# Spreading softmax weights three neighbours at a time in row groups of TensorE, with products and sums on tiles of three

## The chip, the cores and the metric

The kernel runs on one core of a Trainium2 chip. The metric is the device time of one execution in microseconds (us); the runs of the kernel before took 6155.91, 6143.2 and 6156.27, median 6155.91.

## What is computed

The input is x of 16 images, 56 x 56 pixels, 384 channels, all float32. Two layers follow each other; each adds its result to its input. Before each, a group norm over 32 groups of 12 channels is taken for the whole image. The first layer is a dilated neighbourhood attention: 384 channels are three sets of 128 (dilation 1, 2 and 3), each of four heads of 32 channels, and every pixel attends to nine neighbours.

```python
xn = gn(x);  qkv = einsum('bchw,oc->bohw', xn, w_qkv)      # q, k, v for three dilations d = 1, 2, 3
for each dilation d, head h, pixel n:
    attn[n, k] = sum_c q[c, n] * k[c, n + d*(ky-1, kx-1)] * 32**-0.5     # k = 3*ky + kx, nine neighbours
    attn = softmax over k
    out[c, n]  = sum_k attn[n, k] * v[c, n + d*(ky-1, kx-1)]
x = x + einsum(out, w_proj) + b_proj
x = x + depthwise_3x3(gn(x), sign(clip(w_conv)))           # second layer
```

## The kernel before

**Tiles and stages.** An image is seven chunks of eight rows (448 pixels); there are 112 chunks. Channels lie on the 128 partitions, pixels on the free axis. Three plans work on a chunk at different times. Stage A (`plan_a`) loads x, transposes it (L304), takes statistics and stores the transposed copy in DRAM. Stage B (`plan_b`) is the attention with its output projection. Stage C (`plan_c`) is the convolution and the transposition back.

**Order.** Time is divided into steps, nine to a chunk (`STEP`, L579). `at(when, order, piece)` files each piece of work under a step and a kind (L578: SOFTMAX, SCORE, CONVOLVE, WEIGH, QUERY, QKV, PROJECT, ...), and the pieces are issued in that order. Stage A runs nine chunks ahead of B, C ten behind. Each engine has one queue, in order; the framework fixes the order of the instructions of each engine when the kernel is built, and it may let a later piece pass one that isn't ready: in the trace, the third spread matmul of a step often stands among the projection matmuls that follow it. `in_one_go` (L225) keeps the matmuls of a burst together.

**Stage B of a chunk**, with t0 as its first score step:

- `k_or_v` (L341) projects k and v (L337) and copies them from PSUM with ScalarE into `kv` tiles with a border (L346). K and V share a tile, of which there are three per dilation (`KV_SLOTS`). The rows of the border come from the neighbouring chunk by DMA on the SP queue (L350, L351).
- `score` (L378), steps t0 to t0+8: one VectorE product q x k for three neighbours at once (tile t, 128 x 1344, L387). The products of four neighbours are summed over channels by matmuls of 128 rows and 32 columns (L371), which run in four column groups of the array at once, as do the convolution's (L553).
- `softmax_1`, `softmax_2`, `softmax_3` at t0+9 to t0+11: the scores are transposed by a permutation matrix (L400) to 112 pixels by 108 weights, four times; maximum, difference, exponential, sum, reciprocal and product run on VectorE and ScalarE (L405 to L415) with the nine neighbours innermost. `softmax_3` splits each weight into three bf16 terms, alternating between ScalarE and GpSimd (L422 to L425).
- `turn_weights` (L427), t0+12 to t0+14: for each dilation, four transposes (L430) give a tile of 108 rows (three terms x four heads x nine neighbours) and ScalarE copies it (L436).
- `weigh` (L438), t0+13 to t0+21, three neighbours per step: one bf16 matmul with the matrix `spread` (108 rows, 128 columns, L443) sums the terms of a neighbour's weights and copies each to its head's 32 partitions; VectorE multiplies the result, in PSUM, by the shifted v (L446); GpSimd adds the product to y (L453), eight adds per dilation.
- `out_project` (L459), t0+23 to t0+25: projection of the three y (L467), bias and residual on VectorE (L470), statistics (L473), store.

**Norms.** Once per image and layer, `group_stats` and `spread_stats` (L232 to L273) pass small tiles between TensorE, VectorE and ScalarE in a chain.

**PSUM** has eight banks: four for the shared tag "mt" (projections, transposes, convolution, norms), one for the query, one for the scores, and two for the spread weights ("bc").

```python
pb = ps_bc.tile([P, 512], F32, tag="bc", name="pb_a")
nc.tensor.matmul(pb[:, :PX], spread[:, o, :], had[f"a{g}"], start=True, stop=True)
w = w_p.tile([P, PX], F32, tag="w", name="w")
vw = kv[g][slot][:, 1, ky * d : ky * d + ROWS, kx * d : kx * d + W]
nc.vector.tensor_tensor(rows(w), rows(pb[:, :PX]), vw, ALU.mult)
```

Of the kernel before, what the change touches and what calls it, by code (L numbers as in the profile page):

```python
# [8 lines left out]
F32 = mybir.dt.float32  # L9
BF16 = mybir.dt.bfloat16  # L10
AF = mybir.ActivationFunctionType
# [13 lines left out]
GN_CH = 12  # L25
GN_G = 32
NR = NG * HEADS * NTAP
KV_SLOTS = 3
TERMS = 3


# [1 line left out]
def dilated_attention_then_binary_conv(  # L33
# [34 lines left out]
    DIL = (1, 2, 3)  # L68
    K3 = 3 * HD

    xf = x.rearrange("b h w c -> b (h w) c")
    of = out.rearrange("b h w c -> b (h w) c")

    const = ctx.enter_context(tc.tile_pool(name="const", bufs=1))
    ps_mt = ctx.enter_context(tc.tile_pool(name="ps_mt", bufs=4, space=PSUM))
    ps_q = ctx.enter_context(tc.tile_pool(name="ps_q", bufs=1, space=PSUM))
    ps_s = ctx.enter_context(tc.tile_pool(name="ps_s", bufs=1, space=PSUM))
    ps_bc = ctx.enter_context(tc.tile_pool(name="ps_bc", bufs=2, space=PSUM))


    ident = const.tile([P, P], F32, name="ident")
# [9 lines left out]
    for h in range(HEADS):  # L91
        nc.gpsimd.memset(sel[h * HD : (h + 1) * HD, SEL0 + h : SEL0 + h + 1], 1.0)

    perm = const.tile([P, NG, HEADS, NTAP], F32, name="perm")
    nc.gpsimd.memset(perm, 0.0)
    for p in range(NG * NTAP):
        g, o = divmod(p, NTAP)
        nc.gpsimd.affine_select(
            out=perm[:, g, :, o], in_=perm[:, g, :, o], compare_op=ALU.not_equal, fill=1.0,
            base=-(32 * (p % 4) + 4 * (p // 4)), pattern=[[-1, HEADS]], channel_multiplier=1,  # L100
        )
    permf = perm.rearrange("p g h o -> p (g h o)")


    gsel = const.tile([P, NG, GN_G], F32, name="gsel")
# [16 lines left out]
    wprojT = const.tile([P, NG, C], F32, name="wprojT")  # L122
    bias = const.tile([P, NG], F32, name="bias")

    spread = const.tile([NR, NTAP, P], BF16, name="spread")

    kdiag = const.tile([K3, 3, NG * NQ, HD], F32, name="kdiag")
    with tc.tile_pool(name="setup", bufs=1) as setup:
# [28 lines left out]
        nc.tensor.transpose(pt[:, :NG], b_in, ident[:NG, :NG])  # L157
        nc.vector.tensor_copy(bias, pt[:, :NG])

        spread_f = setup.tile([NR, NTAP, P], F32, name="spread_f")  # L160
        nc.gpsimd.memset(spread_f, 0.0)
        for t in range(TERMS):
            nc.gpsimd.affine_select(
                out=spread_f.rearrange("r o (h d) -> r o h d", h=HEADS),
                in_=spread_f.rearrange("r o (h d) -> r o h d", h=HEADS),
                compare_op=ALU.not_equal, fill=1.0, base=-t * HEADS * NTAP,
                pattern=[[-1, NTAP], [-NTAP, HEADS], [0, HD]], channel_multiplier=1,
            )
        nc.vector.tensor_copy(spread, spread_f)


# [28 lines left out]
    xn_p = ctx.enter_context(tc.tile_pool(name="xn_p", bufs=3))  # L200
    xr_p = ctx.enter_context(tc.tile_pool(name="xr_p", bufs=2))
    t_p = ctx.enter_context(tc.tile_pool(name="t_p", bufs=3))
    w_p = ctx.enter_context(tc.tile_pool(name="w_p", bufs=5))
    y_p = ctx.enter_context(tc.tile_pool(name="y_p", bufs=5))
    s_p = ctx.enter_context(tc.tile_pool(name="s_p", bufs=1))
    a_p = ctx.enter_context(tc.tile_pool(name="a_p", bufs=4))
    z_p = ctx.enter_context(tc.tile_pool(name="z_p", bufs=3))
    x1_p = ctx.enter_context(tc.tile_pool(name="x1_p", bufs=2))
    o_p = ctx.enter_context(tc.tile_pool(name="o_p", bufs=2))
# [1 line left out]


    kv = []
    for g, d in enumerate(DIL):
        kv.append([])
        for s in range(KV_SLOTS):
            t = const.tile([P, 2, ROWS + 2 * d, W + 2 * d], F32, name=f"kv_{g}_{s}")
            nc.gpsimd.memset(t[:, :, :, 0:d], 0.0)
            nc.gpsimd.memset(t[:, :, :, W + d : W + 2 * d], 0.0)
            kv[g].append(t)  # L220

    def rows(ap):
        return ap.rearrange("p (r w) -> p r w", w=W)

    def in_one_go(matmuls):  # L225

# [54 lines left out]
    def at(when, order, piece):  # L281

        pieces.setdefault((when, order), []).append(piece)
# [37 lines left out]
    def plan_b(m, t0):  # L321

        b, c = divmod(m, NCH)
        slot, prev = m % KV_SLOTS, (m - 1) % KV_SLOTS
        had = {}

        def load_x():
# [12 lines left out]

        def k_or_v(g, which):  # L341

            d, cur, bef = DIL[g], kv[g][slot][:, which], kv[g][prev][:, which]
            pk = ps_mt.tile([P, 512], F32, tag="mt", name="pkv")
            project(pk, (1 + which) * C + g * P)
            nc.scalar.copy(cur[:, d : d + ROWS, d : d + W], rows(pk[:, :PX]))  # L346
            if c == 0:
                nc.gpsimd.memset(cur[:, 0:d, :], 0.0)
            else:
                nc.sync.dma_start(cur[:, 0:d, :], bef[:, ROWS : ROWS + d, :])  # L350
                nc.sync.dma_start(bef[:, ROWS + d : ROWS + 2 * d, :], cur[:, d : 2 * d, :])  # L351
            if c == NCH - 1:
                nc.gpsimd.memset(cur[:, ROWS + d : ROWS + 2 * d, :], 0.0)
# [24 lines left out]
        def score(i):  # L378

            g, ky = divmod(i, 3)  # L380
            d = DIL[g]
            qg = rows(had["q"][:, :PX])
            q3 = bass.AP(qg.tensor, qg.offset, [qg.ap[0], (0, 3), *qg.ap[1:]])
            kw = kv[g][slot][:, 0, ky * d : ky * d + ROWS, 0:W]
            k3 = bass.AP(kw.tensor, kw.offset, [kw.ap[0], (d, 3), *kw.ap[1:]])
            t = t_p.tile([P, 3, PX], F32, tag="t", name="t")
            nc.vector.tensor_tensor(t.rearrange("p k (r w) -> p k r w", w=W), q3, k3, ALU.mult)  # L387
            ready.extend((i * 3 + kx, t[:, kx, :]) for kx in range(3))
            if len(ready) >= NQ or i == 8:
                score_round()  # L390

        NH = NSUB * NG * HEADS

        def softmax_1():

# [2 lines left out]
            pt = ps_mt.tile([P, 512], F32, tag="mt", name="pt_s")  # L398
            for s in range(NSUB):
                nc.tensor.matmul(  # L400
                    pt[:SUB, s * NR : (s + 1) * NR], sT[:, s * SUB : (s + 1) * SUB], permf, start=True, stop=True
                )
            pt3 = pt[:SUB, : NSUB * NR].rearrange("p (h o) -> p h o", o=NTAP)
            mx = s_p.tile([SUB, NH], F32, tag="mx", name="mx")
            nc.vector.reduce_max(mx, pt3, axis=AX.X)  # L405
            had["e"] = e = s_p.tile([SUB, NH, NTAP], F32, tag="e", name="e")
            nc.vector.tensor_tensor(e, pt3, mx.unsqueeze(2).to_broadcast([SUB, NH, NTAP]), ALU.subtract)
            nc.scalar.activation(e, e, AF.Exp, scale=SCALE)

        def softmax_2():  # L410
            e = had["e"]
            sm = s_p.tile([SUB, NH], F32, tag="sm", name="sm")
            nc.vector.reduce_sum(sm, e, axis=AX.X)
            nc.vector.reciprocal(sm, sm)
            nc.vector.tensor_tensor(e, e, sm.unsqueeze(2).to_broadcast([SUB, NH, NTAP]), ALU.mult)  # L415

        def softmax_3():

            ef = had.pop("e").rearrange("p (s h) o -> p s (h o)", s=NSUB * NG)
            had["e3"] = e3 = s_p.tile([SUB, NSUB * NG, TERMS, HEADS * NTAP], BF16, tag="e3", name="e3")  # L420
            rest = s_p.tile([SUB, NSUB * NG, HEADS * NTAP], F32, tag="rest", name="rest")
            nc.scalar.copy(e3[:, :, 0], ef)  # L422
            nc.gpsimd.tensor_tensor(rest, ef, e3[:, :, 0], ALU.subtract)  # L423
            nc.scalar.copy(e3[:, :, 1], rest)
            nc.gpsimd.tensor_tensor(e3[:, :, 2], rest, e3[:, :, 1], ALU.subtract)  # L425

        def turn_weights(g):  # L427
            pa = ps_mt.tile([P, 1024], BF16, tag="mt", name="pa")
            for s in range(NSUB):
                nc.tensor.transpose(  # L430
                    pa[:NR, s * SUB : (s + 1) * SUB],
                    had["e3"][:, s * NG + g].rearrange("p t m -> p (t m)"),
                    ident_h[:SUB, :SUB],
                )
            had[f"a{g}"] = aT = a_p.tile([NR, PX], BF16, tag="aT", name="aT")
            nc.scalar.copy(aT, pa[:NR, :PX])  # L436

        def weigh(p):  # L438

            g, o = divmod(p, NTAP)  # L440
            d, (ky, kx) = DIL[g], divmod(o, 3)
            pb = ps_bc.tile([P, 512], F32, tag="bc", name="pb_a")
            nc.tensor.matmul(pb[:, :PX], spread[:, o, :], had[f"a{g}"], start=True, stop=True)  # L443
            w = w_p.tile([P, PX], F32, tag="w", name="w")
            vw = kv[g][slot][:, 1, ky * d : ky * d + ROWS, kx * d : kx * d + W]
            nc.vector.tensor_tensor(rows(w), rows(pb[:, :PX]), vw, ALU.mult)  # L446
            if o == 0:
                had["w0"] = w
                return
            if o == 1:  # L450
                had[f"y{g}"] = y_p.tile([P, PX], F32, tag="y", name="y")
            y = had[f"y{g}"]
            nc.gpsimd.tensor_tensor(y, had["w0"] if o == 1 else y, w, ALU.add)  # L453

        def load_residual():
            had["xr"] = xr = xr_p.tile([P, NG, PX], F32, tag="xr", name="xr")
# [37 lines left out]
        at(t0 + 9, SOFTMAX, softmax_1)  # L494
        at(t0 + 10, SOFTMAX, softmax_2)
        at(t0 + 11, SOFTMAX, softmax_3)
        for g in range(NG):
            at(t0 + 12 + g, SOFTMAX, lambda g=g: turn_weights(g))
        for p in range(NG * NTAP):
            at(t0 + 13 + p // 3, WEIGH, lambda p=p: weigh(p))  # L500
        at(t0 + 19, LOADS, load_residual)
        for j in range(NG):
            at(t0 + 23 + j, PROJECT, lambda j=j: out_project(j))
# [111 lines left out]
```

## Time and profile before

| what | value |
|---|---|
| median of the three runs | 6155.91 us |
| profiled execution's own time | 6148.66 us |
| its span, first to last instruction | 6146.7 us |
| mean granted TensorE clock | 0.961 |
| busy: TensorE matmul | 5892.8 us (96%) |
| busy: VectorE | 4420.6 us (72%) |
| busy: GpSimd | 3364.3 us (55%) |
| busy: ScalarE | 2270.5 us (37%) |
| DMA queue q1, share of 16 engines | 48.8% |
| spread matmuls L443 | 3024, 929.5 us busy, 360 ns each |
| products with v, L446 | 3024, 1797.4 us busy, 616 ns each |
| adds to y, L453 | 2688, 3057.9 us busy, 1137 and 1139 ns each |
| transposes of weights, L430 | 1344, 139.9 us busy |

The busy time of an engine counts each moment once, so overlapping matmuls add up to less than count times duration. Matmuls are pipelined: the duration of a row contains the way through the array, and the distance from one start to the next is what a matmul keeps the engine. PEld is the loading of weights, which overlaps with matmuls. The first spread matmul starts 157 us after the span's beginning and the last ends at 5948 us; before and after that only stages A and C and the setup have work.

### The profile page before, as it was taken

What the parts mean: (1) busy time and instruction counts of PE and PEld (TensorE: products, weight loads), DVE (VectorE), ACT (ScalarE), POOL (GpSimd) and SP (SyncE); (2) the same over time, 40 slices, a digit from 0 to 9 for tenths busy, and PEclk for the clock granted to TensorE, in tenths of its full rate; (3) what the DMA queues carried; (4) which work ended last, traced back from release to release, by engine and by line L of the source; (5) the groups of instructions that cost most, each with busy time, mean ns of one, the idle gap of its engine ahead of it and who ended that gap; (6) DMA issues with size and microseconds to landing.
All of it is one profiled execution on the core that took longest, in us unless ns stands there. A gap on an engine that the chain in (4) does not pass through costs nothing. (4 is left out here: it accounts for less than half of the span.)

```text
span 6146.7 us, 90026 instructions
## 1 busy us (share of the span) xinstructions
PE 5892.8 (96%) x30933; PEld 2720.9 (44%) x30933; DVE 4420.6 (72%) x6431; ACT 2270.5 (37%) x4025; POOL 3364.3 (55%) x3375
## 2 busy tenths in 40 slices
PE   6989999999999999999999999999999999999986
PEld 3434444444444444444444444444444444444432
DVE  3767777777777777777777777777777777777760
ACT  2222333333333333334333333333334333333334
POOL 1656555555555555555555556555555555555650
PEclk7999999999999999999999999999999999999985
DMA  4323445554555455545554555555455554444445
GB/s 149 105 69 102 138 132 150 147 148 141 140 149 146 136 152 141 146 136 147 152 143 137 142 148 142 143 146 148 140 140 149 150 149 139 133 131 115 125 131 143
DMA packets 675072, 848.03 MB, mean 138 GB/s; under 512 B 179507, under 2 KB 674614, under 8 KB 674614
## 3 DMA queue, kind: packets, MB, share of 16 engines
q1 hardware_dynamic: 670608, 841.67, 48.8%
q8 instruction: 244, 4.00, 0.3%
q14 instruction: 214, 1.75, 0.1%
q10 hardware_dynamic: 4006, 0.61, 0.1%
HBM read 539.11 MB, written 231.21 MB: 125 GB/s over the span
## 5 line engine op out<-in xcount | busy, mean ns | idle before, releaser
L453 POOL TENSOR_TENSOR y<-y,w 128x448 f32<-128x448 f32 x2352 | 2675.0, 1137 | 1227.8 <-DVE w L446 1085.8
L446 DVE TENSOR_TENSOR w<-pb_a,kv 128x448 f32<-128x448 f32 x3024 | 1797.4, 616 | 479.0 <-PE pb_a L443 468.4
L337 PE MATMUL pkv<-xn,wqkvT 128*128 128x448 f32 x4032 | 1641.9, 542 | 0.0
L387 DVE TENSOR_TENSOR t<-pq,kv 128x1344 f32<-128x1344 f32 x1008 | 1545.9, 1547 | 86.6 <-PE pq L337 70.2
L337 PEld LDWEIGHTS pkv<-xn,wqkvT 128*128 128x128 f32 x4032 | 762.2, 190 | 622.7 <-issue 592.7
L536 ACT ACTIVATE z<-z,mrz 96x448 f32<-96x448 f32 x1344 | 939.2, 757 | 124.7 <-DMA z<-x1d 99.2
L553 PE MATMUL pc<-z,kdiag 96*32 96x440 f32 (+1 forms) x8064 | 924.3, 561 | 54.2 <-ACT z L536 32.0
L443 PE MATMUL pb_a<-aT,spread 108*128 108x448 bf16 x3024 | 929.5, 360 | 47.9 <-DVE w L446 38.5
L346 ACT COPY kv<-pkv 128x448 f32<-128x448 f32 x672 | 358.6, 534 | 1607.8 <-PE pkv L337 1607.4
L337 PE MATMUL pq<-xn,wqkvT 128*128 128x448 f32 x2016 | 904.5, 560 | 0.0
L467 PE MATMUL po<-y,wprojT 128*128 128x448 f32 x2016 | 828.6, 539 | 1.7 <-POOL y L453 1.7
L371 PE MATMUL ps<-t,sel 128*32 128x448 f32 x6048 | 781.1, 570 | 31.7 <-DVE var L255 15.9
L453 POOL TENSOR_TENSOR y<-w 128x448 f32<-128x448 f32 x336 | 382.9, 1139 | 724.6 <-DVE w L446 685.7
L560 DVE TENSOR_TENSOR x<-pc,x 128x448 f32<-128x448 f32 x336 | 209.8, 624 | 582.6 <-PE pc L553 581.9
L443 PEld LDWEIGHTS <-spread 108*128 108x128 bf16 x3024 | 238.0, 98 | 786.7 <-issue 730.1
L467 PEld LDWEIGHTS po<-y,wprojT 128*128 128x128 f32 x2016 | 382.1, 190 | 337.3 <-issue 305.8
L470 DVE SCALAR_TENSOR_TENSOR xr<-po,bias,xr 128x448 f32<-128x448 f32 x336 | 228.7, 681 | 407.5 <-PE po L467 401.8
L337 PEld LDWEIGHTS pq<-xn,wqkvT 128*128 128x128 f32 x2016 | 400.1, 200 | 260.8 <-issue 230.2
L553 PEld LDWEIGHTS pc<-z,kdiag 96*32 96x32 f32 x8064 | 265.7, 113 | 554.3 <-issue 463.3
L423 POOL TENSOR_TENSOR rest<-e,e 112x432 f32<-112x432 f32 x112 | 114.2, 1019 | 391.4 <-ACT e L422 375.1
L308 ACT COPY xa<-pt_x 128x448 f32<-128x448 f32 x336 | 179.0, 534 | 362.5 <-PE pt_x L304 355.0
L333 ACT ACTIVATE xn<-xn,mr 128x448 f32<-128x448 f32 x336 | 231.4, 751 | 202.8 <-DMA xn<-xd 145.9
(90 smaller groups left out, 3363.0 us busy)
## 6 DMA issues: line engine op xcount, KB each, us to landing
z<-x1d SPq DMA_DIRECT2D x912, 224.0 KB, 4.0
xin<-in_x_dram SPq DMA_DIRECT2D x112, 672.0 KB, 6.5
xd<-xa SPq DMA_DIRECT2D x336, 224.0 KB, 2.3
xn<-xd SPq DMA_DIRECT2D x112, 672.0 KB, 4.5
xr<-xd SPq DMA_DIRECT2D x112, 672.0 KB, 4.3
x1d<-xr SPq DMA_DIRECT2D x112, 672.0 KB, 3.1
x<-x1d SPq DMA_DIRECT2D x112, 672.0 KB, 5.0
out_dram<-osb SPq DMA_DIRECT2D x448, 168.0 KB, 2.3
```

Of the source, the lines that this page charges most:

```text
L333: nc.scalar.activation(xj, xj, AF.Identity, bias=mr0[b][:, j, 0:1], scale=mr0[b][:, j, 1:2])
L337: nc.tensor.matmul(dst[:, :PX], wqkvT[:, cc, o0 : o0 + P], had["xn"][:, cc, :], start=(cc == 0), stop=(cc == NG - 1))
L346: nc.scalar.copy(cur[:, d : d + ROWS, d : d + W], rows(pk[:, :PX]))
L371: return nc.tensor.matmul(had["ps"][32 * j : 32 * j + 32, :PX], sel[:, s0 : s0 + 32], tk, start=(i == 0), stop=(p + NQ >= NG * NTAP),)
L387: nc.vector.tensor_tensor(t.rearrange("p k (r w) -> p k r w", w=W), q3, k3, ALU.mult)
L443: nc.tensor.matmul(pb[:, :PX], spread[:, o, :], had[f"a{g}"], start=True, stop=True)
L446: nc.vector.tensor_tensor(rows(w), rows(pb[:, :PX]), vw, ALU.mult)
L453: nc.gpsimd.tensor_tensor(y, had["w0"] if o == 1 else y, w, ALU.add)
L467: nc.tensor.matmul(po[:, :PX], wprojT[:, g, j * P : (j + 1) * P], had[f"y{g}"], start=(g == 0), stop=(g == NG - 1))
L470: nc.vector.scalar_tensor_tensor(xr[:, j, :], po[:, :PX], bias[:, j : j + 1], xr[:, j, :], op0=ALU.add, op1=ALU.add)
L536: nc.scalar.activation(z[:, q], z[:, q], AF.Identity, bias=mr1[b][:, j, q, 0:1], scale=mr1[b][:, j, q, 1:2])
L553: return nc.tensor.matmul(pcr[q * HD : (q + 1) * HD, :, lo:hi], kdiag[:, kx, j * NQ + q, :], rows(z[:, q])[:, :, lo + kx - 1 : hi + kx - 1 ...
```

## The change

For each dilation and each of its three rows of neighbours (ky), the three neighbours kx are now handled together:

- The weights of a chunk are laid out by neighbour, then dilation, then head, padded to 32 groups of four (`NPAD`). Three bf16 terms of two such groups fill 24 of 32 rows, so that a transposed tile of 128 rows holds eight groups in four row groups of 32. There are four such tiles per chunk (`turn_weights(u)`) where there were three.
- `weigh(i)` issues three matmuls of 24 rows and 128 columns, each in another row group of TensorE and into another PSUM bank, as one burst. The three neighbours of a burst are placed so that their row groups differ.
- One VectorE product of 128 x 1344 replaces three of 128 x 448. GpSimd adds whole tiles of three, and at the end of a dilation adds the three parts to y: two adds of 1344 elements and two of 448 per dilation.
- PSUM: "bc" becomes one buffer of three banks, "mt" falls from four buffers to three.
- Maximum and sum over the neighbours now read with the neighbours outermost (stride 12), and `ew` and `e3`, the weights and their terms, are single tiles for the whole run, zeroed once. The split works on 512 columns instead of 432, in runs of eight.
- K and V have tiles of their own, two slots for K and three for V.

```diff
+NPAD = 32
+K_SLOTS, V_SLOTS = 2, 3
...
+    def place(p):
+
+        g, o = divmod(p, NTAP)
+        return NG * o + g
...
-    ps_mt = ctx.enter_context(tc.tile_pool(name="ps_mt", bufs=4, space=PSUM))
+    ps_mt = ctx.enter_context(tc.tile_pool(name="ps_mt", bufs=3, space=PSUM))
...
-    ps_bc = ctx.enter_context(tc.tile_pool(name="ps_bc", bufs=2, space=PSUM))
+    ps_bc = ctx.enter_context(tc.tile_pool(name="ps_bc", bufs=1, space=PSUM))
...
-    spread = const.tile([NR, NTAP, P], BF16, name="spread")
+    spread = const.tile([P, 2, P], BF16, name="spread")
...
+    ew = const.tile([SUB, NSUB * NPAD * HEADS], F32, name="ew")
+    e3 = const.tile([SUB, NSUB, NPAD // 8, P], BF16, name="e3")
...
         def softmax_2():
-            e = had["e"]
-            sm = s_p.tile([SUB, NH], F32, tag="sm", name="sm")
-            nc.vector.reduce_sum(sm, e, axis=AX.X)
+            sm = s_p.tile([SUB, NSUB, GH], F32, tag="sm", name="sm")
+            nc.vector.reduce_sum(sm, by_neighbour(weights).rearrange("p s o k -> p s k o"), axis=AX.X)
             nc.vector.reciprocal(sm, sm)
...
         def softmax_3():
...
+            rest = s_p.tile([SUB, NSUB * NPAD * HEADS], F32, tag="rest", name="rest")
+            eights = "p (u k) -> p u k"
+            e8 = ew.rearrange(eights, k=8)
+            r8 = rest.rearrange(eights, k=8)
+            term = [e3.rearrange("p s u (r k) -> p (s u r) k", r=4)[:, :, 8 * t : 8 * t + 8] for t in range(TERMS)]
+            nc.scalar.copy(term[0], e8)
+            nc.gpsimd.tensor_tensor(r8, e8, term[0], ALU.subtract)
+            nc.scalar.copy(term[1], r8)
+            nc.gpsimd.tensor_tensor(term[2], r8, term[1], ALU.subtract)
...
+        def turn_weights(u):
             pa = ps_mt.tile([P, 1024], BF16, tag="mt", name="pa")
             for s in range(NSUB):
+                nc.tensor.transpose(pa[:, s * SUB : (s + 1) * SUB], e3[:, s, u], ident_h[:SUB, :SUB])
+            had[f"a{u}"] = aT = a_p.tile([P, PX], BF16, tag="aT", name="aT")
+            nc.scalar.copy(aT, pa[:, :PX])
+
+        def weigh(i):
+
+            g, ky = divmod(i, 3)
+            pb = ps_bc.tile([P, 3, 512], F32, tag="bc", name="pb_a")
+
+            def copy(kx):
+                v = place(3 * i + kx)
+                lo = 32 * (v // 2 % 4)
+                rows_of = slice(lo, lo + 2 * TERMS * HEADS)
+                return nc.tensor.matmul(
+                    pb[:, kx, :PX], spread[rows_of, v % 2, :], had[f"a{v // 8}"][rows_of, :], start=True, stop=True
+                )
+
+            in_one_go([lambda kx=kx: copy(kx) for kx in (2, 0, 1)])
+            w = w_p.tile([P, 3, PX], F32, tag="w", name="w")
+            nc.vector.tensor_tensor(
+                w.rearrange("p k (r w) -> p k r w", w=W),
+                pb[:, :, :PX].rearrange("p k (r w) -> p k r w", w=W), three(kv[1][g][m % V_SLOTS], DIL[g], ky), ALU.mult,
+            )
+            if ky == 0:
+                had["w0"] = w
                 return
+            w0 = had["w0"]
+            nc.gpsimd.tensor_tensor(w0, w0, w, ALU.add)
+            if ky == 2:
+                had[f"y{g}"] = y = y_p.tile([P, PX], F32, tag="y", name="y")
+                nc.gpsimd.tensor_tensor(y, w0[:, 0], w0[:, 1], ALU.add)
+                nc.gpsimd.tensor_tensor(y, y, w0[:, 2], ALU.add)
...
-        for g in range(NG):
-            at(t0 + 12 + g, SOFTMAX, lambda g=g: turn_weights(g))
-        for p in range(NG * NTAP):
-            at(t0 + 13 + p // 3, WEIGH, lambda p=p: weigh(p))
+        for u in range(NPAD // 8):
+            at(t0 + 12 + u // 2, SOFTMAX, lambda u=u: turn_weights(u))
+        for i in range(9):
+            at(t0 + 13 + i, WEIGH, lambda i=i: weigh(i))
```

## The prediction

> **What bounds the kernel now.** I first read the busy table and the costliest groups of the page, and then cut the steady part into chunks at the first L443 matmul of each. 100 of the 112 chunks (10 to 109) run in the steady state; a chunk lasts 50.2 us in five of the seven of an image, and 57.5 to 58.9 us in the two that hold a group norm. The windows view of one plain chunk (columns: window, length, then busy us of PE, PEld, DVE, ACT, POOL, clock, DMA share, GB/s):
>
> ```profile
> 2963.46:3013.65 50.19, 50.13 (x274) 23.31 (x272) 38.28 (x53) 19.16 (x36) 29.30 (x27) 1.00 0.52 149
> ```
>
> TensorE is busy for all of it at full clock; VectorE has 12 us to spare, GpSimd 21, ScalarE 31. Busy PE need not be PE at its peak, so I added up distances between matmul starts. The timeline of PE (start, duration, group):
>
> ```profile
> 3023.44 0.95 PE L371 MATMUL ps<-t,sel 128*32 128x448 f32 x6
> 3024.32 0.55 PE L443 MATMUL pb_a<-aT,spread 108*128 108x448 bf16 x2
> 3024.71 1.67 PE L337 MATMUL pkv<-xn,wqkvT 128*128 128x448 f32 x4
> 3026.21 0.35 PE L443 MATMUL pb_a<-aT,spread 108*128 108x448 bf16 x1
> 3026.41 3.17 PE L337 MATMUL pkv<-xn,wqkvT 128*128 128x448 f32 x8
> 3029.41 2.42 PE L467 MATMUL po<-y,wprojT 128*128 128x448 f32 x6
> ```
>
> Eight projection matmuls take 3.00 us, 0.375 each. A spread matmul occupies TensorE for 0.188 us (the median distance to a next matmul of the same array shape), though its row says 360 ns: the rest is pipeline. The four narrow matmuls of a score burst start 7 ns apart and share one stream. Where the array's shape changes (128*32 to 128*128 or back) the distance is 469 to 472 ns where 376 is the stream: 0.095 us more. With these, the 269 matmuls of a plain chunk and its 16 changes of shape fill the 50.2 us; there is no hole. What TensorE loses, the kernel gains, while nobody makes it wait.
>
> How near it is to waiting is seen where the softmax weights arrive (ends of the chain for one chunk):
>
> ```profile
> 3002.26 1.03 POOL L423 TENSOR_TENSOR rest<-e,e 112x432 f32<-112x432 f32 x1 [4.39 <-ACT e L422]
> 3004.33 1.03 POOL L425 TENSOR_TENSOR e<-rest,e 112x432 bf16<-112x432 f32 x1
> 3006.84 0.36 PE L430 MATMUL pa<-ident_h,e 112*108 112x112 bf16 x4
> ```
>
> L425 ends at 3005.36 and TensorE reaches its transposes at 3006.84: 1.5 us of slack, and over all plain chunks it is 1.0 to 1.5 us. In the early chunks, which have no convolution to fill TensorE, it is gone; the waits from 300 to 600 us say so:
>
> ```profile
> PE pa L430 <- POOL e L425: 15.9, 5, 4.1
> ```
>
> Each such stall is followed by 3.4 to 10 us at half clock.
>
> **What the Trainium skill says.** "TensorEngine Tiling (Array Packing)", Key Properties: changing the tiling mode drains TensorE. The trace agrees: 0.095 us per change. "TensorE: Matmul & The Clock Gate", Measured speedup vs the span model: tiles in different row groups overlap, a few ns apart; four row tiles of 512 columns gained 3.07 times. Column tiles do so here (7 ns); no row tile is in this trace. "SBUF — State Buffer", Who interferes with whom: a VectorE instruction with two SBUF inputs waits out a GpSimd instruction that reads SBUF. The trace agrees: the 32x1 product at L260 took 838 ns on average, its like at L259 143.
>
> **The change, part by part** (per plain chunk, TensorE time unless said).
>
> 1. *27 spread matmuls become 9 bursts of three in different row groups.* Removed: 27 x 0.188 = 5.08 us. Added: 9 x (0.188 + 2 x 0.007) = 9 x 0.202 = 1.82. **-3.26 us.** Row tiles are not in the trace: full overlap gives 0.202 per burst, none gives 3 x 0.188 = 0.564. The skill's 3.07 of 4 would be about 0.25. I take 0.202, as column tiles show.
> 2. *Changes of shape.* The burst is 32*128, a third shape. I took the matmul order of a plain chunk and put each burst where its first matmul stands: six bursts lie between a narrow group (scores, convolution) and a wide one, +1 each; three between wide ones, +2 each; one single matmul between convolution and scores goes away, -2. Net 10 x 0.095 = **+0.95 us** (8 to 18 changes: 0.76 to 1.7; nothing, if a row-tiled burst costs no change).
> 3. *Transposes and permutation.* Four units, not three, of four transposes: 4 x 0.050 = +0.20. The permutation streams 128 columns for 108: 8 x (0.116 - 0.098) = +0.14.
>    Sum: 50.19 - 3.26 + 0.95 + 0.34 = 48.22, **-1.97 us a chunk**; on 100 steady chunks **-197 us**. For the first ten I count nothing: their stalls, not their matmuls, set the pace; the last two have too little to matter.
> 4. *One buffer of three banks for the spread weights.* A burst waits until the product of the burst before has been read. From the trace: first w start of a step plus 1.55 us (the wide t row at L387, 1547 ns, same shape) lies a median of 1.4 us before the next burst, and later than it in 14 of 1008 steps, 3 us in total. Taken at zero. PE's small waits today on w (L443 <- L446, 38.5 us) are not counted as gain: in exchange all three banks are now read at once.
> 5. *ps_mt falls from four buffers to three.* I set each tile's first matmul against the end of the reading of the tile three before it: 33 of 2374 late, **+23 us** in total (18 of it where transposes of weights follow output transposes). It could be zero if the order adapts, or double, since a fourth weight tile is added. Behind a waiting PE instruction everything on PE is queued.
> 6. *VectorE:* 27 x 0.616 = 16.6 becomes 9 x 1.547 = 13.9 us: -2.7, off the path (38.3 of 48). The two softmax reductions now read every twelfth element: unknown, between the 0.60 us of today and twice that; I take today's plus a half, +0.6 us on the softmax chain. Subtraction and scaling keep rows of 12 and are left at 0.60.
> 7. *GpSimd:* eight adds of 1.137 per group become two of 1344 elements and two of 448. A wide add costs between 3.0 us (drawn from 1137 ns at 448 to the 4497 ns at 2048 that "GPSIMD Engine Reference", 3.1, states; an estimate) and 3.4 (three narrow ones). 3 x (6.0 + 2.3) = 24.9 for 27.3: 27 us of 48 with softmax, not the bound. But a VectorE op with two SBUF inputs now waits out 3.0 us: in each norm L249, L260, L262 and L263 lose about 2.0 us today; by length-weighted waits (mean remaining 1.24 us for 0.57) that becomes 4.4. The scores' products queue behind them on VectorE and TensorE behind those (14 waits of about 1 us on L255 and on L257). 28 norms x 2.4 = 67; I count half, **+34 us**, since TensorE has other work for part.
> 8. *Split of the weights:* L423 and L425 go from 432 to 512 elements, 1.02 to 1.21 (unless runs of 8 elements cost more: up to 1.8); L422 and L424 from 0.55 to about 0.62; one more L436 copy, 0.54 us on an idle ScalarE. On the chain: +0.5.
> 9. *The chain's slack.* 1.0 to 1.5, less 0.7 because TensorE runs 21 us of distance 4% quicker, less 0.5 and 0.6 for 8 and 6, plus 0.7 because nothing is summed for a first neighbour row (the add between L423 and L425 goes, 0.4) and VectorE has 0.3 less in the way: about 0 us left. I take **+15 us** of small waits.
> 10. *Setup:* more, smaller selections and zero fills on GpSimd (24 at about 0.29 for 3 at 1.42; a dozen of 0.15): **+5 us**. Separate K and V tiles with two and three slots: the same copies and transfers on the SP queue; a K slot is rewritten four steps after its scores. Zero.
>
> **Sum:** -197 + 23 + 34 + 15 + 5 = -120 us on the profiled execution's 6148.7 (span 6146.7): 6029. The median shown, 6155.9, is 7 us above that execution: between 6029 and 6036; I say **6030**. Bounds of the terms that stay in this case: changes free, mt and norm at zero: about 5930; bursts of 0.25 us, 18 changes: about 6110.
>
> **The rivals.**
> *A, the rows don't overlap (0.12).* Every burst takes 0.564 us, so the 3.26 us come back and the changes of shape remain: -120 + 326 = +206, about **6355: slower**. It decides from a burst of 0.202 + 1.20/9 = 0.335 us upwards. Against: columns overlap, and the skill has it for rows; for: no row of this trace shows it.
> *B, the softmax chain ends last (0.15).* If item 6, 8 or a wide add between L423 and L425 (3.0 us, in one queue) takes 1.5 us more than I counted, TensorE waits about 2 us in every plain chunk, and, as in the early chunks, half clock follows and costs 3.4 more: 48.2 + 5.4 = 53.6, +3.4 on 71 plain chunks, the 29 others (9 us of slack) keep their -2: +241 - 57 + 77 = +261, about **6410: slower**. The cliff begins where TensorE idles some 0.8 us of a 3.4 us window (windows ahead of half clock are busy 0.4 to 0.8).
> *C, the buffers give it back (0.10).* mt and bc stalls of 1.2 us a chunk: 6150, **no change**.
>
> **Chances.** Forecast 0.63 (own range 5930 to 6110), A 0.12, B 0.15, C 0.10. The range of eight in ten reaches from 5930 to A's 6355, leaving out B and a small tail below. Faster by over 0.2%, about what a measurement can tell: 0.63 + 0.04 of C = 0.67; same 0.05; slower 0.28.
>
> **What would show it.** In the profile after: plain chunks of 48.2 us; bursts with starts 7 ns apart and about 0.30 to the next wide matmul; L443's busy down to a third; VectorE's w row at 1.55; wide adds at 3.0; L249 and L260 longer. Wrong, if a burst's distances are 188 each (A), if the transposes of weights wait for GpSimd in most chunks and the clock's mean falls below 0.95 (B), or if PE waits for ScalarE's and VectorE's copies (C).

## The result and the profile after

| | before | changed |
|---|---|---|
| median | 6149.56 us (6141.31 to 6156.27) | 6190.24 us (6188.65 to 6191.66) |
| ratio to before | | 1.0067 (95% interval 1.0049 to 1.0084) |
| profiled execution's span | 6146.7 us | 6186.9 us |
| mean granted TensorE clock | 0.961 | 0.943 |

The median before is over one run more than at the start. The forecast was 6030; the kernel became 0.7% slower. The burst itself does what it was meant to do. From the page of the changed kernel, the groups of the wide add, of the wide product and of the burst (busy, mean ns, idle before):

```profile
L486 POOL TENSOR_TENSOR w<-w 128x1344 f32<-128x1344 f32 x672 | 2045.8, 3044 | 1500.9 <-DVE w L478 1368.6
L478 DVE TENSOR_TENSOR w<-pb_a,v 128x1344 f32<-128x1344 f32 x1008 | 1556.9, 1545 | 293.0 <-PE pb_a L472 288.7
...
L472 PE MATMUL pb_a<-aT,spread 24*128 24x448 bf16 x3024 | 378.8, 364 | 97.1 <-DVE w L478 84.3
```

The spread matmuls' busy time fell from 929.5 to 378.8 us, with the same number of matmuls; the product takes 1545 ns and the wide add 3044, as assumed. The timeline of PE in a plain chunk shows a burst:

```profile
2996.65 0.36 PE L472 MATMUL pb_a<-aT,spread 24*128 24x448 bf16 x3
2996.95 2.52 PE L359 MATMUL pq<-xn,wqkvT 128*128 128x448 f32 x6
2999.31 1.04 PE L429 MATMUL pt_s<-perm,sT 128*112 128x128 f32 x8
```

Three matmuls in 0.36 us, and 0.30 us from the first to the next wide one: they overlap. But six projection matmuls now take 2.36 us to the next group, where six starts 0.376 us apart make 2.26; more on that below.

The windows of chunks, from the first spread matmul of one to that of the next, tell where the time went (window, length, busy us of PE, PEld, DVE, ACT, POOL, clock, DMA share, GB/s). Before, the two norm chunks of one image:

```profile
3064.19:3121.76 57.57, 54.40 (x298) 25.67 (x295) 42.83 (x68) 20.88 (x38) 30.72 (x33) 0.97 0.41 111
3221.99:3280.03 58.04, 55.61 (x298) 25.59 (x295) 41.58 (x66) 22.34 (x39) 29.27 (x30) 0.94 0.45 129
```

After, a plain chunk and the two norm chunks:

```profile
2972.55:3021.37 48.82, 48.68 (x276) 21.97 (x276) 36.72 (x35) 19.94 (x37) 27.09 (x15) 1.00 0.54 153
3070.19:3135.69 65.50, 57.06 (x312) 26.10 (x311) 43.12 (x50) 21.83 (x39) 30.20 (x22) 0.90 0.39 108
3231.07:3295.78 64.71, 56.74 (x299) 26.10 (x298) 42.17 (x48) 22.62 (x40) 28.27 (x22) 0.87 0.37 104
```

A plain chunk takes 48.8 us for 50.2. The two norm chunks grew by 7.9 and 6.7 us and lose clock: the first holds the norm of the first layer, the second that of the second layer. In this image 1.4 us are won in each of five plain chunks (one of them, after a norm, takes 46.6 and wins two more), and 14.6 are lost in the two others.

In the first norm chunk TensorE waits (start, duration, group, idle before and its releaser):

```profile
3110.30 0.37 PE L472 MATMUL pb_a<-aT,spread 24*128 24x448 bf16 x3 [0.78 <-DVE w L478]
3111.77 0.96 PE L394 MATMUL ps<-t,sel 128*32 128x448 f32 x8 [1.10 <-DVE var L280]
3119.03 1.72 PE L394 MATMUL ps<-t,sel 128*32 128x448 f32 x8 [6.31 <-DVE var L284]
```

A hole of 6.3 us; before, the longest wait of a score burst on a norm was 1.1 us. (The named releaser is the last link of the norm's chain; the burst needs a score product t, queued on VectorE among those links.) VectorE's timeline over that hole:

```profile
3111.63 0.14 DVE L280 RECIPROCAL var<-var 32x1 f32<-32x1 f32 x1
3111.70 1.53 DVE L478 TENSOR_TENSOR w<-pb_a,v 128x1344 f32<-128x1344 f32 x1
3113.15 0.27 DVE L282 TENSOR_TENSOR var<-var 32x1 f32<-32x1 f32 x1
3113.35 1.54 DVE L409 TENSOR_TENSOR t<-pq,k 128x1344 f32<-128x1344 f32 x1
3114.82 2.69 DVE L283 TENSOR_TENSOR var<-var 32x1 f32<-32x1 f32 x1
3117.44 1.54 DVE L409 TENSOR_TENSOR t<-pq,k 128x1344 f32<-128x1344 f32 x1
3118.91 0.13 DVE L284 TENSOR_SCALAR var<-var 32x1 f32<-32x1 f32 x1
3119.07 0.85 DVE L285 TENSOR_TENSOR pair<-var 32x1 f32<-32x1 f32 x1
```

and the same links before:

```profile
3106.85 0.14 DVE L257 RECIPROCAL var<-var 32x1 f32<-32x1 f32 x1
3107.03 0.15 DVE L259 TENSOR_TENSOR var<-var 32x1 f32<-32x1 f32 x1
3107.21 1.07 DVE L260 TENSOR_TENSOR var<-var 32x1 f32<-32x1 f32 x1
3108.31 0.14 DVE L261 TENSOR_SCALAR var<-var 32x1 f32<-32x1 f32 x1
3108.49 1.00 DVE L262 TENSOR_TENSOR pair<-var 32x1 f32<-32x1 f32 x1
```

Two things differ. Before, these links stand back to back; after, a product of 1.55 us stands between almost every two (QUEUE). And L283 takes 2.69 us for a product of 32 numbers, while GpSimd is in a wide add (LOCK):

```profile
3114.47 3.03 POOL L486 TENSOR_TENSOR w<-w 128x1344 f32<-128x1344 f32 x1
```

L283 ends when this add ends. So it is with the links of two tensor inputs that took over 0.3 us: all 90 after and all 87 before end within 0.03 us of the end of a GpSimd operation.

In the norm of the second layer a product stood between the links before the change, too, but one of 0.6 us:

```profile
3240.27 0.14 DVE L257 RECIPROCAL var<-var 32x1 f32<-32x1 f32 x1
3240.34 0.59 DVE L446 TENSOR_TENSOR w<-pb_a,kv 128x448 f32<-128x448 f32 x1
3240.87 0.14 DVE L259 TENSOR_TENSOR var<-var 32x1 f32<-32x1 f32 x1
3240.93 0.60 DVE L446 TENSOR_TENSOR w<-pb_a,kv 128x448 f32<-128x448 f32 x1
3241.47 0.76 DVE L260 TENSOR_TENSOR var<-var 32x1 f32<-32x1 f32 x1
```

and after, with products of 1.54 us:

```profile
3251.94 0.14 DVE L280 RECIPROCAL var<-var 32x1 f32<-32x1 f32 x1
3252.01 1.53 DVE L409 TENSOR_TENSOR t<-pq,k 128x1344 f32<-128x1344 f32 x1
3253.47 1.68 DVE L282 TENSOR_TENSOR var<-var 32x1 f32<-32x1 f32 x1
3255.07 1.54 DVE L478 TENSOR_TENSOR w<-pb_a,v 128x1344 f32<-128x1344 f32 x1
3256.54 0.14 DVE L283 TENSOR_TENSOR var<-var 32x1 f32<-32x1 f32 x1
```

Summed from the trace over 25 steady norms, from the last bn_aggr to the copy of mr: the chain lasts 22.5 us before and 28.7 after; other work between its links takes 15.4 and 20.6 us; the links themselves 4.3 and 5.9. So the chain's growth of 6.2 us is 5.2 of queue and 1.6 of lock, less some shorter pauses. The queue holds fewer pieces but longer ones: 16 operations between the links of a norm for 20, of 1.29 us for 0.77 on average. Of the 5.2 us, 2.0 are products with v (six of 1344 elements for twelve of 448) and 3.1 are two more score products, whose size did not change.

From 3113.1 us on, within the hole, the clock is halved for 13.7 us; between 1000 and 5600 us there were 154 us of half clock before and 386 after.

### The profile page after: what moved, and what is told of

It reads as the page before. It is cut to its first block, busy times and chain, and to the rows that moved or that the text cites. A ratio compares the mean times of both kernels' runs of the same rounds, so it can differ in the third digit from the quotient of the medians.

```text
span 6186.9 us, 84655 instructions
## 1 busy us (share of the span) xinstructions
PE 5772.2 (93%) x31381; PEld 2600.1 (42%) x31381; DVE 4312.9 (70%) x4415; ACT 2344.1 (38%) x4137; POOL 3162.6 (51%) x2066
## 5 line engine op out<-in xcount | busy, mean ns | idle before, releaser
L486 POOL TENSOR_TENSOR w<-w 128x1344 f32<-128x1344 f32 x672 | 2045.8, 3044 | 1500.9 <-DVE w L478 1368.6
L478 DVE TENSOR_TENSOR w<-pb_a,v 128x1344 f32<-128x1344 f32 x1008 | 1556.9, 1545 | 293.0 <-PE pb_a L472 288.7
L409 DVE TENSOR_TENSOR t<-pq,k 128x1344 f32<-128x1344 f32 x1008 | 1543.4, 1549 | 216.3 <-PE pq L359 214.5
L590 PE MATMUL pc<-z,kdiag 96*32 96x440 f32 (+1 forms) x8064 | 943.2, 571 | 53.8 <-ACT z L573 32.1
L369 ACT COPY v<-pkv 128x448 f32<-128x448 f32 x336 | 180.0, 536 | 1595.7 <-PE pkv L359 1595.5
L359 PEld LDWEIGHTS pq<-xn,wqkvT 128*128 128x128 f32 x2016 | 359.4, 194 | 347.1 <-issue 347.1
L472 PE MATMUL pb_a<-aT,spread 24*128 24x448 bf16 x3024 | 378.8, 364 | 97.1 <-DVE w L478 84.3
L452 POOL TENSOR_TENSOR rest<-ew,e 112x512 f32<-112x512 f32 x112 | 129.9, 1160 | 597.2 <-ACT e L451 525.6
L490 POOL TENSOR_TENSOR y<-y,w 128x448 f32<-128x448 f32 x336 | 382.8, 1139 | 26.3
L489 POOL TENSOR_TENSOR y<-w 128x448 f32<-128x448 f32 x336 | 381.9, 1137 | 22.5
L472 PEld LDWEIGHTS <-spread 24*128 24x128 bf16 x3024 | 105.1, 91 | 599.6 <-issue 567.7
```

Source lines behind the costliest of these rows:

```text
L359: nc.tensor.matmul(dst[:, :PX], wqkvT[:, cc, o0 : o0 + P], had["xn"][:, cc, :], start=(cc == 0), stop=(cc == NG - 1))
L472: return nc.tensor.matmul(pb[:, kx, :PX], spread[rows_of, v % 2, :], had[f"a{v // 8}"][rows_of, :], start=True, stop=True)
L478: nc.vector.tensor_tensor(w.rearrange("p k (r w) -> p k r w", w=W), pb[:, :, :PX].rearrange("p k (r w) -> p k r w", w=W), three(kv[1][g][m ...
L486: nc.gpsimd.tensor_tensor(w0, w0, w, ALU.add)
L489: nc.gpsimd.tensor_tensor(y, w0[:, 0], w0[:, 1], ALU.add)
L490: nc.gpsimd.tensor_tensor(y, y, w0[:, 2], ALU.add)
```

## The experiments

QUEUE and LOCK are to be told apart; that norms are the whole loss, and the two terms of the prediction about the buffers, are tested too. All times are medians; the ratio is to the kernel before on the same chip.

**e1: narrow adds.** GpSimd's wide add in three pieces of 448.

```diff
-            nc.gpsimd.tensor_tensor(w0, w0, w, ALU.add)
+            for kx in range(3):
+                nc.gpsimd.tensor_tensor(w0[:, kx], w0[:, kx], w[:, kx], ALU.add)
```

> The changed kernel with each wide GpSimd add of 1344 elements cut into three of 448; nothing else is touched. Two theories for the norm chunks, which went from about 58 to 65 us: LOCK: VectorE's small products of the norm wait out GpSimd's 3.04 us adds (in the changed kernel they lose 3.6 us per norm, 2.0 before); with adds of 1.14 us that falls to about 2, and with the half clock behind the stall 2 to 5 us per norm come back on 27 norms: 6060 to 6130 us. QUEUE: what stretches the chain is the wide VectorE products (1.55 us each) standing between its links, not the lock: 6160 to 6200 us, since the adds' total even grows by 0.4 us each.

Measured: 6182.62, ratio 1.0056 (1.0041 to 1.0071). The links fell from 5.9 to 4.8 us per norm, the work between them stayed at 20.6. The length of the adds alone is worth little; the time lies in QUEUE's range.

**e2: no second tensor input.** The norm's small products take a per-partition scalar instead.

```diff
-        nc.vector.tensor_mul(t, r, r)
-        nc.vector.tensor_mul(t, t, v)
+        nc.vector.tensor_scalar(t, r, r, None, op0=ALU.mult)
+        nc.vector.tensor_scalar(t, t, v, None, op0=ALU.mult)
```

(and likewise for pair; the two operations on dev become six.)

> The changed kernel with the norm's two-tensor products on VectorE (L271, L272, L282, L283, L285, L286) written as tensor_scalar with one tensor and a per-partition scalar, so that no second tensor input comes from SBUF; the wide adds stay. LOCK: the 3.6 us of waiting per norm vanish, and with less half clock 4 to 8 us per norm: 5980 to 6090 us. QUEUE: at most the waiting itself, without the clock: 6110 to 6190 us.

Measured: 6128.83, ratio 0.9969 (0.9957 to 0.9981), 61 us less than changed. The links shrink from 5.9 to 3.1 us, so the waiting is gone, and the chain is 1.9 us shorter; 20.7 us of other work still stand between the links, and the norm chunks still take 61 to 64 us. The lock is real, and what it is worth alone is a third of what the best version below gets back.

**e3: the norm first.** The chain of group_stats and spread_stats built inside `with tc.high_priority():`, nothing else.

> The changed kernel with the norm's chain built at high priority, so that its links stand back to back in VectorE's queue instead of having a wide product between each two; operations and sizes are the same, and the wide adds stay. QUEUE: the norm chunks return to about 57 us, 27 x 7.5 us less: 5970 to 6020 us. LOCK: the links still wait out wide adds, up to 3 us each: 6100 to 6190 us.

Measured: 6098.64, ratio 0.9917 (0.9901 to 0.9932), 92 us less than changed: more than e2, but at the edge of LOCK's range and far from QUEUE's. The windows of the two norm chunks of an image say why:

```profile
3011.34:3079.18 67.84, 59.49 (x312) 26.54 (x312) 40.76 (x50) 22.05 (x39) 30.32 (x22) 0.90 0.36 101
3174.56:3229.03 54.47, 51.39 (x300) 23.84 (x300) 39.95 (x48) 22.86 (x40) 28.25 (x22) 1.00 0.50 139
```

In the second, the order came out with the links L281 to L287 (the former L280 to L286) back to back; their beginning:

```profile
3189.96 1.53 DVE L480 TENSOR_TENSOR w<-pb_a,v 128x1344 f32<-128x1344 f32 x1
3191.42 0.14 DVE L281 RECIPROCAL var<-var 32x1 f32<-32x1 f32 x1
3191.60 0.73 DVE L283 TENSOR_TENSOR var<-var 32x1 f32<-32x1 f32 x1
3192.36 0.15 DVE L284 TENSOR_TENSOR var<-var 32x1 f32<-32x1 f32 x1
```

That chunk takes 54.5 us at full clock, for 64.7. In the first of the two the wide products still stand between the links, and it takes 67.8. It is so in all 14 steady images: 54 to 56 us for the one, 66 to 68 for the other. One kernel thus shows both orders, with the same wide products and wide adds.

**e4: e2 and e3 together.**

> Both at once: the norm's chain at high priority and without second tensor inputs. Both theories: the norm chunks fall to about 55 us or less and the kernel to 5920 to 5990 us. If one cause alone were enough, this equals the better of the two single runs within 20 us.

Measured: 6002.11, ratio 0.9757 (0.9741 to 0.9774): 188 us less than changed, where the single edits gave 61 and 92. They add, and 35 us more; the expected 5920 to 5990 us were not reached. The wide products, wide adds, bursts and buffers are all still there.

**e5: narrow products.** The product with v in three pieces, the wide adds kept:

```diff
-            nc.vector.tensor_tensor(
-                w.rearrange("p k (r w) -> p k r w", w=W),
-                pb[:, :, :PX].rearrange("p k (r w) -> p k r w", w=W), three(kv[1][g][m % V_SLOTS], DIL[g], ky), ALU.mult,
-            )
+            v3 = three(kv[1][g][m % V_SLOTS], DIL[g], ky)
+            for kx in range(3):
+                nc.vector.tensor_tensor(rows(w[:, kx]), rows(pb[:, kx, :PX]), v3[:, kx], ALU.mult)
```

> The changed kernel with the wide product with v cut into three of 448 pixels (616 ns each, 0.3 us more per step), bursts, buffers and wide adds unchanged. QUEUE, in the form that the length of what stands between two links is what counts: 6080 to 6140 us. If the wide product is only one of several (scores' products of 1.55 us stand there too, and the scheduler puts something between any two links): 6160 to 6200. LOCK or the single buffer of three banks: no gain, 6180 to 6210.

Measured: 6009.80, ratio 0.9773 (0.9758 to 0.9787), 180 us less than changed by this edit alone, though VectorE has more to do (37.9 us per plain chunk for 36.7). That is more than I expected of any theory. The windows of a plain and the two norm chunks:

```profile
2937.55:2986.51 48.96, 48.78 (x276) 21.97 (x275) 37.86 (x53) 19.86 (x37) 28.15 (x16) 1.00 0.55 156
2986.51:3042.75 56.24, 52.94 (x300) 24.02 (x299) 43.18 (x68) 21.66 (x39) 30.61 (x22) 0.97 0.40 113
3143.12:3198.08 54.96, 52.43 (x299) 24.18 (x298) 41.97 (x66) 22.86 (x40) 28.22 (x22) 0.97 0.49 136
```

and VectorE's queue in the first of the norm chunks:

```profile
3026.87 0.15 DVE L280 RECIPROCAL var<-var 32x1 f32<-32x1 f32 x1 [0.18 <-ACT var L279]
3027.05 2.75 DVE L282 TENSOR_TENSOR var<-var 32x1 f32<-32x1 f32 x1
3029.83 0.15 DVE L283 TENSOR_TENSOR var<-var 32x1 f32<-32x1 f32 x1
3030.01 0.14 DVE L284 TENSOR_SCALAR var<-var 32x1 f32<-32x1 f32 x1
3030.19 0.15 DVE L285 TENSOR_TENSOR pair<-var 32x1 f32<-32x1 f32 x1
```

The lock is as bad as ever (L282: 2.75 us), yet the links stand together again. The work between links is back at 15.1 us, the chain at 20.6, half clock at 165 us. So shorter products change the order that the framework finds, not just what one link waits for; no run has the short products in the changed kernel's order, so the two are not told apart. TensorE's longest waits on VectorE fall too; from the waits between 1000 and 5600 us (total, times, longest), changed kernel and then e5:

```profile
PE ps L394 <- DVE var L284: 89.5, 25, 6.3
PE pb_a L472 <- DVE w L478: 64.2, 25, 4.2
```

```profile
PE pb_a L472 <- DVE w L480: 33.7, 25, 1.4
PE ps L394 <- DVE var L278: 22.6, 25, 1.1
```

The second line of the changed kernel is the single buffer of three banks: in the other norm of an image the burst waits 4.2 us for a product that is queued among the links. It falls with the order as well: in e3, with the same buffer and the wide products, it is 0.8 us at longest. How much of e5 it is by itself was not tried.

**n1, n2: no norms.** Mean and rstd constant in both kernels.

```diff
+        mr = st_p.tile([P, NG, 2], F32, tag="mr", name="mr", bufs=4)
+        nc.gpsimd.memset(mr[:, :, 0:1], 0.0)
+        nc.gpsimd.memset(mr[:, :, 1:2], 1.0)
```

> The changed kernel without the two norms' chains: mean and rstd are constants (0 and 1) written by GpSimd, the statistics of the chunks are still taken; so the norms are left out of the computation. If the loss lies in the norms alone, every chunk takes 46.6 to 48.8 us and the kernel 5740 to 5800 us; beside the kernel before without norms a ratio of 0.965 to 0.98. If something else of the change costs time too (three buffers, the chain of the softmax), the ratio is 0.985 or more.

> The kernel before without the norms' chains, in the same way: 50.2 us in every chunk, so 6147 less 28 norms of about 8 us: 5900 to 5940 us.

Measured: 5726.05 (ratio 0.9313, 0.9297 to 0.9328) and 5909.75 (0.9609, 0.9594 to 0.9623); the one over the other is 0.969, as expected, though the first lies 14 us below its range. Nearly every steady chunk is 48.8 and 50.2 us (91 and 87 of 100). So the change wins 184 us outside the norms. The norms cost 240 us before (6149.56 - 5909.75) and 464 in the changed kernel (6190.24 - 5726.05): 224 more. (That 224 - 184 gives the measured difference of 40 follows from the subtraction and proves nothing; that the loss goes with the norms is shown by the 0.969.)

**b4: both edits of the norm in the kernel before.**

> The kernel before with both edits of the norm (high priority, no second tensor input). Its norm chunks lose 8 us against a plain one, of which 2 us are lock and about 1.1 per stall: 6030 to 6090 us. The changed kernel with the same edits, 6002, is then 0.5 to 1.5% ahead; if it were behind, the change would not pay even with its new stalls removed.

Measured: 6170.96, ratio 1.0033 (1.0020 to 1.0046): 20 us slower, an expectation missed. The work between the links hardly fell (15.0 us), and the chunk of the second layer's norm takes 60 us where it took 58 to 59; why was not followed. So the edits cure a stall that only the changed kernel has, and e4 is 169 us ahead of its counterpart.

**e6, e7, e8: e5 with e2, with e2 and e3, and with e1.**

> Products with v of 448 pixels (as in e5) and the norm's products without a second tensor input (as in e2), the rest as changed. If queue and lock are separate costs, the second edit is worth here what it was worth alone, 54 to 61 us: 5940 to 5965 us. If e5 had already taken the lock's cost with it (the links no longer meet the adds), 5990 to 6015.

> Products of 448, no second tensor inputs, and the norm's chain at high priority. If the queue's order still costs after e5 (15 us of other work stand between the links), another 20 to 80 us: 5870 to 5945 us. If e5's order is already as good as the early norm gets, 5940 to 5990; high priority made the kernel before 20 us slower, so a loss against e6 is possible too.

> Products with v and GpSimd's adds both in pieces of 448: of the change's wide tiles only the burst remains. Alone, the narrow adds were worth 7 us (e1). Independent costs: 5995 to 6015 us. If the lock counts more once the links stand closer: 5950 to 5990.

Measured: 6004.28 (0.9765, 0.9751 to 0.9780), 6001.58 (0.9759, 0.9743 to 0.9775), 6006.22 (0.9767, 0.9753 to 0.9782). All lie 4 to 8 us below e5, at e4's level: once the hole of 6 us is gone, removing the lock or putting the norm first is worth next to nothing more. e6 and e8 came out as expected; e7 reached neither of its two ranges (5870 to 5990). These versions beat both kernels, by 2.4% against the kernel before.

**b5: three buffers of mt in the kernel before.** `bufs=3` for `ps_mt`.

> The kernel before with three buffers of the tag mt in place of four, nothing else: tests the prediction's 23 us for it. From the overlap counted in the trace: 6165 to 6180 us. If the order adapts: 6145 to 6155. If TensorE has to wait for copies in most steps: above 6250.

Measured: 6176.80, ratio 1.0047 (1.0032 to 1.0062): +28 us, against 23 counted from the trace. TensorE's new wait is where the count had it:

```profile
PE pa L430 <- ACT osb L567: 15.4, 12, 1.8
```

The transposes of the weights wait for the copy of the output transposes three tiles back.

## Why the prediction was wrong

**The step that failed is item 7, the price of the norm: 34 us counted, 224 measured.** I had the mechanism of the lock (VectorE's two-input products waiting out wide adds; L283 is at 1337 ns on average, its like before at 838), and put 2.4 us per norm on it, of which I counted half. That part was of the right size: the lock grew by 1.6 us per norm, and taking all of it away (e2) gave 61 us. What I left out is the other wide operation. In item 6 I took the wide product as a pure gain, 2.7 us less of an engine off the path, and named no place where its length counts. It is off the path in plain chunks. In the norm's chain VectorE carries a link of 0.15 us again and again, and whatever stands between two links delays both the chain and the score products behind it: 16 pieces of 1.29 us in place of 20 of 0.77. That the width of this product brings it about is shown by e5: cutting it takes 180 us away. How much of that is the length itself, and how much the other order that the framework then finds, stays open; e3 shows that the order alone, with every tile wide, can be worth 10 us in one norm chunk.

**No rival had this.** I gave "slower" 0.28, but only by A, B and a tail; the way it came stands in none of them. One sign that I had put down for B, a mean clock below 0.95, did appear (0.943); without the norms the clock was 0.98 (n1).

**The half clock was tied to the wrong place.** I knew that a hole in TensorE's work is followed by half clock and used it only for rival B, the softmax chain. In the norm chunks it came: 386 us of half clock for 154. In 110 of the additional 232 us TensorE was idle and lost nothing by it; in the other 122 it worked at half clock, which is a loss of about 61 us. The larger part is the holes themselves: between 1000 and 5600 us TensorE is idle for 213 us, and was for 70 before. (An estimate from the clock record and TensorE's busy time; no run has the hole without the half clock.)

**Rival B did not happen where I put it.** The chain of the softmax became 0.8 us shorter (20.2 us for 21.0 from the last score to the first transpose) and kept 0.1 to 0.2 us of slack in most plain chunks, close to the "about 0" of item 9. The strided sum cost 918 ns for 593, inside my bound; the strided maximum from PSUM 599 for 597, nothing.

**Item 1 was right.** Bursts start 3 to 4 ns apart, rival A is out.

**Item 2 was right in count and short in price.** A plain chunk has 25 changes of shape, nine more than before; I said ten. Leaving the row-tiled shape costs 0.100 us at once (288 ns to the next matmul for 188), and 0.104 more on the second float32 projection matmul (480 ns for 376), six times a chunk; with smaller ones on transposes (0.05 us on those of the output) it comes to about 0.7 us that I had not.

**The sum of the rest came out, by two misses that cancel.** Outside the norms I had -197 + 23 + 15 + 5 = -154 us, and 184 were measured. Steady chunks gave 1.4 us each and not 1.97; the first chunks, which I counted at zero, went from 49 or 50 us to 42.9. There, between 300 and 600 us, the waits of the transposes on GpSimd fell from 4.1 to 1.1 us at longest; what shortened them was not tried. The bounds of my range do not come out of the terms named with them, which give about 5880 and 6150 us in place of 5930 and 6110; 6190 lies outside both.

**Items 4 and 5.** The three mt buffers cost 28 us in the kernel before, as counted. The single buffer of three banks costs nothing in plain chunks, but 4.2 us once per image in a norm: my count of slack was taken over steps of the kernel before, whose norm chunks were short.

**Rival C** has no part in the changed kernel: TensorE's waits for ScalarE's copies come to less than 2 us in the whole run. **Item 10** was low by little: the first spread matmul starts at 165.5 us for 157.2, 8 us later for 5.

## What to carry to other kernels

Price a wider operation also by the chain of small dependent operations that shares its queue, not only by the busy time it saves: operations may stand between two links of a chain, and there fewer, longer pieces delayed it more than many short ones. A hole in the bounding engine that comes twice per image can cost more than the gain of all other stages, in part because half clock goes with it. When a change packs work into larger pieces, try it with each piece cut again: here the packed matmuls gain 2.3% as soon as the product that reads them is narrow.

## What the runs showed of the hardware that was not expected

- Row-tiled bursts of three (24 rows, 128 columns, three PSUM banks) start 3 to 4 ns apart, closer than the column tiles' 7 ns, but leaving them costs 0.100 us, and 0.104 us more on the second float32 projection matmul that follows.
- A VectorE sum over float32 in SBUF with a stride of 48 bytes took 918 ns for 593 without; a maximum over PSUM with the same stride 599 ns for 597.
- A VectorE product of two tensors of 32 numbers took up to 2.75 us while GpSimd was in a wide add; as tensor_scalar with a per-partition scalar it took 0.2 us (e2).
- A wide GpSimd add costs 3044 ns for three of 1137: 11% less. The split of the weights in runs of eight ran at 1160 ns for 512 elements, so the short runs cost nothing visible (1019 ns for 432).
